# M2 accumulated onto M1's copy in PSUM, M5 kept in C22's place, W1's blocks read into `tv`, and U's dots moved behind its C22 addition

## The chip, the cores and the metric

The kernel runs on one core of a Trainium2 chip. The metric is the device time of one execution in microseconds; lower is better. Before the change it is 2272.84 us, the median of three runs (2270.68 to 2274.14).

## The reference, cut to what matters

The program runs two graph layers on 32 independent graphs ("batches" below) of 512 nodes with 512 features. All numbers are fp32.

```python
h = relu(layernorm(x))
deg = adj.sum(-1)
x = x + relu(concat([h, (adj @ h) / max(deg, eps)]) @ W.T)            # layer 0
h = relu(layernorm(x))
q, k = split(h @ Wqk)
v = h @ Wv
w = scale * mask * ((q * (adj @ (k * mask[:, None]))).sum(-1))        # one score per node
x = x + softmax(w)[:, None] * v                                       # layer 1
```

The kernel rearranges this. Layer 0 becomes `Y = h @ W2` and `o = h @ W1 + (adj/deg) @ Y`. In layer 1 the two weight halves of `Wqk` are multiplied once at the start, so `T = h1 @ (Wq Wk^T)`, `V = h1 @ Wv`, `U = adj/deg @ (h1 * mask)`, and a node's score is the dot product of its row of `T` with its row of `U`, times its degree and mask.

## The kernel before

**Work.** Every 512x512 product is done by one level of Strassen-Winograd: seven products M1 to M7 of 256x256 blocks in place of eight, and additions that combine them. A result has four blocks C11, C12, C21, C22. The sums of operand blocks are written into extra "slots" next to the four blocks (`left_sums`, `right_sums`), by VectorE (DVE).

**Stages.** For each batch `i` four stages run one after the other on TensorE (PE): `layer0_y` makes Y, `layer0_out` makes `o` and adds it to x, `layer1_tv` makes T and V of the batch before, and `layer1_u` makes U. T and V have a second level of Strassen over the weight side, and lie together in one tile `tv` of [128, 2, 2, 14, 128]: the third index is 0 for T and 1 for V. Here "h1 WqWk" in the change's name is the T half, `tv[:, :, 0]`.

**`product`** (line 118) is the common body of Y, o and U. In the kernel before it runs M1, M2, M6, M5, M7, M3, M4. M1, M6, M7 and M4 add up in one PSUM bank `pp`; M2 has a bank `pr`; M5 and M3 share a bank `pq`. Each running sum that a result block needs is copied out of PSUM by ScalarE (ACT, `copy`, line 100), and the block's other part is added by DVE (`add`, line 94; `sub` is line 97). For C22, both M5 and the sum after M7 are copied out by ACT and then added by DVE from SBUF. In `layer0_out` each M has two terms, first `h @ W1`, then `(adj/deg) @ Y`, eight TensorE instructions each; in the trace every matmul of the source shows up as two.

**Order of the work.** Nothing is scheduled by the compiler: the order of the instructions on each engine is the order in which the program emits them. A stage is a Python generator that yields after each group of matmuls, and `run(phase, n, plan)` calls, after step `n` of the stage, whatever `plan.at(n, ...)` has put there, in the order in which it was put. So a plan decides where an addition, a reduction or a load stands in the queue of its engine. Each of these queues (PE, DVE, ACT, GpSimd = POOL, and SP, which issues nearly all loads and stores) runs in order.

**The attention of the batch before** is done by a class `Post`: `recombine` (seven additions on `tv`), `dot` (line 611, four dots of rows of T and U), `scores` and `maximum` (DVE lines 616 and 617, then a reduction over partitions on GpSimd, line 620), `shift` (L623), `exponents` (ACT, L626), `row_sum` (DVE L629, then a second reduction over partitions on GpSimd, L630), `weights` (DVE, L633 and L634), and then V is scaled (`apply`, ACT L638), x is added by a DMA with accumulation that GpSimd issues (`add_x1`, L645), and the rows are stored. `FrontA.factor` (L337) is a small product of degrees and mask on GpSimd; GpSimd also does the power in `variance` (L246).

In `layer0_y` of batch i+1 the plan puts `shift` at step 0, `exponents` at 1, `row_sum` at 2, `FA[i].factor` at 2 (put there after `row_sum`), `weights` at 4, and the recombination of V at 3 to 6. In `layer1_u` the plan puts the recombination of T at 1 and 2, two dots each at 3 and 4, `scores` and `maximum` at 5.

**W1.** The seven blocks of W1 with their sums are kept in device memory[...]; `Stream` reads them again for each batch into four rotating buffers of their own, four at the start of `layer1_u` and three during `layer0_out`.

**PSUM.** All eight banks come from one pool, `ps_m`.

Of the kernel before, what the change touches and what calls it, by code (L numbers as in the profile page):

```python
# [11 lines left out]
F32 = mybir.dt.float32  # L12
# [4 lines left out]
P = 128  # L17
# [5 lines left out]
def kernel(  # L23
# [32 lines left out]

    nc = tc.nc
    B, N, F = x.shape  # L60
    C = N // P
# [7 lines left out]
    big = ctx.enter_context(tc.tile_pool(name="big", bufs=1))  # L69
    small = ctx.enter_context(tc.tile_pool(name="small", bufs=2))  # L70
    dram = ctx.enter_context(tc.tile_pool(name="dram", bufs=2, space=bass.MemoryType.DRAM))
    ps_m = ctx.enter_context(tc.tile_pool(name="ps_m", bufs=8, space=bass.MemoryType.PSUM))


    LEFT = {1: 0, 2: 1, 3: 2, 4: 3, 5: 4, 6: 5, 7: 6}
# [3 lines left out]

    PLACE = {2: 0, 3: 1, 4: 2, 7: 3, 1: 4, 6: 5, 5: 6}  # L80
    AT = {p: j for j, p in PLACE.items()}
    ORDER = [1, 2, 6, 5, 7, 3, 4]

    def slots(tag, bufs, name, pool=None):
        return (pool or big).tile([P, 7, 2, H], F32, tag=tag, bufs=bufs, name=name)

    def block(name):
        return big.tile([P, 2, H], F32, tag="tmp", bufs=4, name=name)

    def mm_tile(name):  # L90
        return ps_m.tile([P, 2, H], F32, tag="m", name=name)

    def add(o, a, b, on=None):
        (on or nc.vector).tensor_tensor(o, a, b, op=ALU.add)  # L94
# [4 lines left out]
    def copy(o, i):  # L99
        nc.scalar.activation(o, i, AF.Copy)  # L100
# [14 lines left out]
    def of(t):  # L115
        return lambda i: t[:, i]

    def product(name, terms, place, finish):

        def m(k, p, first):
            n = 0
            for lt, rt in terms:
                right = rt(k)
                for rc in range(2):
                    for dk in range(2):
                        nc.tensor.matmul(  # L130
                            p[:, rc, :],
                            lt[:, LEFT[k], dk, ts(rc, P)],
                            right[:, dk, :],
                            start=first and n == 0,
                            stop=True,
                            skip_group_check=True,
                        )
                        n += 1
                yield

        pp = mm_tile(f"pp_{name}")
        yield from m(1, pp, True)
        c11 = place(0, 0)
        copy(c11, pp)
        pr = mm_tile(f"pr_{name}")
        yield from m(2, pr, True)
        finish(0, 0, c11, pr, c11)
        yield from m(6, pp, False)
        c12 = place(0, 1)
        copy(c12, pp)  # L150
        pq = mm_tile(f"pq_{name}")
        yield from m(5, pq, True)
        m5 = block(f"m5_{name}")
        copy(m5, pq)
        yield from m(7, pp, False)
        c22 = place(1, 1)
        copy(c22, pp)
        finish(1, 1, c22, m5, c22)
        yield from m(3, pq, False)
        finish(0, 1, c12, pq, c12)  # L160
        yield from m(4, pp, False)
        finish(1, 0, None, pp, None)
# [14 lines left out]
    class Later:  # L177


        def __init__(self, tiles, c):  # L180
            self.tiles, self.c = tiles, c
# [218 lines left out]
    class Stream:  # L400


        def __init__(self):
            self.d = dram.tile([7, P, 2, H], F32, tag="dw1", bufs=1, name="dw1")
            self.tiles = []
            self.n = 0

        def load(self):
            k = ORDER[self.n % 7]
            t = big.tile([P, 2, H], F32, tag="w1", bufs=4, name=f"w1_{self.n}")  # L410
            nc.sync.dma_start(out=t, in_=self.d[RIGHT[k]])
            self.tiles.append((k, t))
            self.n += 1

        def take(self, k):
            want, t = self.tiles.pop(0)
            assert want == k
            return t

    def into(t):  # L420

# [8 lines left out]

    def layer0_y(b):
        y = Y[b] = slots("yh", 1, f"y_{b}")
        return product(f"y_{b}", [(hT, right(w2R))], *into(y))

    def layer0_out(b, w1):
        def place(r, c):
# [14 lines left out]
    def layer1_tv(b):  # L451

        t = TV[b] = tv
        left = H1T[b]

        def m(k, banks, first):
            for half in ((2, 1), (3, 0)):
                for n in half:  # L460
                    if first:
                        banks[n] = mm_tile(f"ptv_{b}_{k}_{n}")
                    for i, p in enumerate(range(2 * n, min(2 * n + 2, 7))):
                        j = AT[p]
                        nc.tensor.matmul(  # L465
                            banks[n][:, :, ts(i, P)],
                            left[:, LEFT[k], LEFT_IN[j], :],
                            mvR[:, RIGHT[k], RIGHT[j], :, :],
                            start=first and i == 0,
                            stop=True,  # L470
                            skip_group_check=True,
                        )
# [12 lines left out]
        def keep(o):  # L485
            return lambda n, p: copy(part(o, n), p)

        def plus(o):
            return lambda n, p: add(part(o, n), p, part(o, n))

        pp, pr, pq, m5 = {}, {}, {}, {}

        def keep5(n, p):
            m5[n] = block(f"m5_tv_{b}_{n}")[:, :, 0:P * min(2, 7 - 2 * n)]
            copy(m5[n], p)

        yield from parts(1, pp, True, keep(0))
        yield from parts(2, pr, True, plus(0))
        yield from parts(6, pp, False, keep(1))
        yield from parts(5, pq, True, keep5)  # L500
        yield from parts(7, pp, False, lambda n, p: add(part(3, n), p, m5[n]))
        yield from parts(3, pq, False, plus(1))
        yield from parts(4, pp, False, keep(2))

    def layer1_one(b, which, held=None):
# [40 lines left out]
        def plus(o):  # L546
            return lambda n, p: add(part(o, n), p, part(o, n))

        pp, pr, pq, m5 = {}, {}, {}, {}

        def keep5(n, p):
            m5[n] = like(n, block(f"m5_w_{which}_{b}_{n}").rearrange("p a f -> p (a f)"))
            copy(m5[n], p)

        yield from parts(1, pp, True, keep(0))
        yield from parts(2, pr, True, plus(0))
        yield from parts(6, pp, False, keep(1))
        yield from parts(5, pq, True, keep5)
        yield from parts(7, pp, False, lambda n, p: add(part(3, n), p, m5[n]))
        yield from parts(3, pq, False, plus(1))  # L560
        yield from parts(4, pp, False, keep(2))

# [16 lines left out]
    class Post:  # L579
# [167 lines left out]
    def start():  # L747
# [42 lines left out]
            for k in range(2):  # L790
                turn_right(s2[h], h, k, w2R)
        for c in range(C):
            v = block(f"h_{c}").rearrange("p a f -> p (a f)")
            nc.scalar.activation(
                in_order(v), natural(X[0][:, c, :]), AF.Relu, scale=t[1][:, c:c + 1], bias=t[2][:, c:c + 1]
            )
            turn_chunk(v, c, "h")
# [7 lines left out]
        rows = {}  # L805

        def scale_a(c):
            rows[c] = block(f"a_{c}").rearrange("p a f -> p (a f)")
            nc.scalar.activation(
                in_order(rows[c]), natural(fa.n[c // 2][:, c % 2, :]), AF.Copy, scale=fa.rdeg[:, c:c + 1]  # L810
            )
# [122 lines left out]
    with tc.manual_schedule(engines=engines):  # L934
        weights, mvR = start()
        post = None
        for i in range(B):
# [4 lines left out]
            if i > 0:  # L942

                p = Plan()
                for n in range(3):
                    p.at(2 * n + 1, stream.load)
                right_y = right_sums(of(Y[i]))
                p.at(0, right_y[0])
                p.at(0, right_y[2])
# [45 lines left out]
                p.at(12, f.stats, 0)  # L995
                p.at(12, f.stats, 1)
                p.at(13, variance, f.t, 0, 2)
                run(layer0_out(i, stream.take), 14, p)


                post = Post(i - 1, F1[i - 1])
# [55 lines left out]
            if more:  # L1057
                p.at(0, f.turn, 0)
                p.at(1, f.turn, 1)
                p.at(2, FA[i + 1].to.read, 0)  # L1060
                p.at(3, FA[i + 1].to.read, 1)
                for n in range(4):
                    p.at(0, stream.load)
            if i == 0:
                fh = FH[2]
                for c in range(C):
# [4 lines left out]
            elif more:  # L1071
                for k in range(7):
                    p.at(1 + k // 4, post.recombine, k, 1, 0)
                for c in range(C):
                    p.at(3 + c // 2, post.dot, c)
                p.at(5, post.scores)
                p.at(5, post.maximum)
                if i == 1:
                    for c in range(C):
                        p.at(3 + c, fa.sum, c)  # L1080
# [24 lines left out]
            if more:  # L1105
# [3 lines left out]
                p.at(3, fb.turn, 1)  # L1109
                p.at(4, fb.sums, 0)  # L1110
                p.at(4, fb.sums, 2)
                p.at(1, load_x, i + 1)
                if i + 2 < B:
                    p.at(5, FH[i + 2].to.read, 0)
                if i > 0:
                    p.at(0, post.shift)
                    p.at(1, post.exponents)
                    p.at(2, post.row_sum)
                    p.at(4, post.weights)
                    for k in range(7):  # L1120
                        p.at(3 + k // 2, post.recombine, k, None, 1)
                p.at(2, FA[i].factor)
# [84 lines left out]
```

## Time and profile before

| | |
|---|---|
| median of three runs | 2272.84 us |
| the profiled execution | 2273.22 us, of which the span from the first to the last instruction is 2271.4 us |
| TensorE clock granted | 0.999 |
| PE busy | 2259.1 us, 99% of the span |
| weight loads of PE busy | 1978.7 us, 87% |
| DVE busy | 1923.6 us, 85% |
| ACT busy | 1025.6 us, 45% |
| POOL busy | 174.8 us, 8% |
| DMA | 463.68 MB, 204 GB/s over the span |

The profile is one execution. Times in it are counted from the first instruction. A busy share is the time in which an engine ran at least one instruction; matmuls overlap each other, so the mean duration of one (379 ns) is longer than the time from one to the next. A timeline row is: start in us, duration in us, engine, source line, operation, output<-input with buffer numbers left out, shapes, how many were merged into the row, and in brackets how long the engine sat idle before it and what ended that. In the list of groups the columns are: line, engine, operation, names, shapes and count, then total busy us and mean ns of one, then the idle time of the engine just before them with what ended most of it.

### The profile page before, as it was taken

To read this page: it belongs to the slowest core of one execution; us is meant where nothing else is said; L and a number is where in the kernel's file an instruction comes from. 1 tells how busy PE (TensorE), PEld (TensorE's weight loads), DVE (VectorE), ACT (ScalarE), POOL (GpSimd) and SP (SyncE) were. 2 spreads that over 40 slices of the span, in tenths; PEclk is the share of its full clock that TensorE was granted. 3 is DMA by queue.
4 is the path that set the end of the run, shared out by engine and by line. 5 is a ranking of instruction groups with operands and counts; after the bars stand their busy time and mean duration, and the time that the engine had idled before them with its cause. 6 is when DMAs were issued, how large, how long until landed. Compare 5 with 4: busy or idle time off the path is not lost.

```text
span 2271.4 us, 32927 instructions
## 1 busy us (share of the span) xinstructions
PE 2259.1 (99%) x10550; PEld 1978.7 (87%) x10550; DVE 1923.6 (85%) x3803; ACT 1025.6 (45%) x1896; POOL 174.8 (8%) x260
## 2 busy tenths in 40 slices
PE   9999999999999999999999999999999999999998
PEld 7788888888888888888888888888888888888897
DVE  7798888888888888888888888888888888888778
ACT  4454443445434554444454344544444543445323
POOL 0000010000100000100000000000000010000000
PEclk9999999999999999999999999999999999999999
DMA  9978787887878777777878888777888787878543
GB/s 222 233 214 246 204 212 193 205 230 206 210 199 202 213 220 207 208 191 207 227 210 205 199 201 218 218 207 202 196 210 225 209 209 193 205 219 217 154 123 96
DMA packets 409773, 463.68 MB, mean 204 GB/s; under 512 B 37729, under 2 KB 271713, under 8 KB 405377
## 3 DMA queue, kind: packets, MB, share of 16 engines
q1 hardware_dynamic: 400192, 428.56, 69.5%
q0 software_dynamic: 8928, 32.51, 8.7%
q8 instruction: 83, 1.36, 0.3%
q14 instruction: 90, 0.73, 0.1%
q10 hardware_dynamic: 480, 0.52, 0.1%
HBM read 293.93 MB, written 167.51 MB: 203 GB/s over the span
## 4 chain that ended last, share of the span: by engine, by line
PE 93%; DMA 3%; DVE 2%; SPq 1%; ACT 0%; issue 0%; DVEq 0%; POOLq 0%; ACTq 0%
PE ptv L465 28%; PE pp_o L130 18%; PE pp_u L130 9%; PE pq_o L130 9%; PE pp_y L130 9%; PE pq_u L130 5%; PE pr_o L130 5%; PE pq_y L130 5%; PE pr_u L130 2%; PE pr_y L130 2%; PE pw L517 1%; DMA a<-in_adj_dram 1%; SPq L212 0%; DVE tv L94 0%; DMA room<-in_L_gnn_Wqk_dram 0%; DVE mv L97 0%
## 5 line engine op out<-in xcount | busy, mean ns | idle before, releaser
L465 PE MATMUL ptv<-mv,h1T 128*128 128x256 f32 x2940 | 639.7, 379 | 0.1
L465 PEld LDWEIGHTS ptv<-mv,h1T 128*128 128x128 f32 x2940 | 558.5, 190 | 76.4 <-DVE xu L444 0.5
L94 DVE TENSOR_TENSOR tv<-tv 128x256 f32<-128x256 f32 (+1 forms) x658 | 326.4, 508 | 13.4 <-ACT tv L100 1.5
L100 ACT ACTIVATE tv<-ptv 128x512 f32<-128x512 f32 (+1 forms) x360 | 184.9, 541 | 262.9 <-PE ptv L465 262.0
L130 PE MATMUL pp_y<-wide 128*128 128x256 f32 x1024 | 242.1, 379 | 1.5 <-ACT y L100 1.2
L130 PE MATMUL pp_u<-h1m,aT 128*128 128x256 f32 x1024 | 242.0, 379 | 0.0
L130 PE MATMUL pp_o<-y,aT 128*128 128x256 f32 x1024 | 241.9, 379 | 0.0
L130 PE MATMUL pp_o<-w,wide 128*128 128x256 f32 x992 | 234.3, 379 | 0.0
L130 PEld LDWEIGHTS pp_y<-wide 128*128 128x128 f32 x1024 | 194.2, 190 | 28.5 <-ACT y L100 1.6
L130 PEld LDWEIGHTS pp_u<-h1m,aT 128*128 128x128 f32 x1024 | 194.4, 190 | 27.0 <-issue 0.7
L130 PEld LDWEIGHTS pp_o<-y,aT 128*128 128x128 f32 x1024 | 194.5, 190 | 26.4
L130 PEld LDWEIGHTS pp_o<-w,wide 128*128 128x128 f32 x992 | 188.5, 190 | 25.6
L100 ACT ACTIVATE o<-pp_o 128x512 f32<-128x512 f32 x96 | 57.2, 596 | 296.0 <-PE pp_o L130 296.0
L100 ACT ACTIVATE y<-pp_y 128x512 f32<-128x512 f32 x128 | 76.3, 596 | 234.5 <-PE pp_y L130 233.4
L94 DVE TENSOR_TENSOR tv<-ptv,tv 128x512 f32<-128x512 f32 x240 | 139.6, 613 | 43.7 <-PE ptv L465 38.4
L97 DVE TENSOR_TENSOR h1T<-h1T 128x512 f32<-128x512 f32 (+2 forms) x193 | 165.8, 873 | 1.2
L100 ACT ACTIVATE xu<-pp_u 128x512 f32<-128x512 f32 x128 | 76.4, 597 | 195.9 <-PE pp_u L130 195.9
L246 POOL TENSOR_TENSOR rstd<-rstd,mhalf 128x2 f32<-128x2 f32 (+1 forms) x96 | 78.7, 820 | 651.0 <-DVE rstd L245 651.0
L130 PE MATMUL pq_y<-wide 128*128 128x256 f32 x512 | 121.0, 379 | 0.0
L130 PE MATMUL pq_o<-y,aT 128*128 128x256 f32 x512 | 121.0, 379 | 0.0
L130 PE MATMUL pq_u<-h1m,aT 128*128 128x256 f32 x512 | 121.0, 379 | 0.0
L94 DVE TENSOR_TENSOR tv<-ptv,m_tv 128x512 f32<-128x512 f32 (+1 forms) x120 | 72.0, 622 | 55.6 <-PE ptv L465 55.1
(130 smaller groups left out, 3269.4 us busy)
## 6 DMA issues: line engine op xcount, KB each, us to landing
w<-dw SPq DMA_DIRECT2D x217, 256.0 KB, 4.3
xu<-in_x_dram SPq DMA_DIRECT2D x128, 256.0 KB, 5.3
a<-in_adj_dram SPq DMA_DIRECT2D x256, 128.0 KB, 3.0
dh1T<-h1m SPq DMA_DIRECT2D x128, 256.0 KB, 3.1
dx<-xu SPq DMA_DIRECT2D x32, 1024.0 KB, 5.1
sh1T<-dh1T SPq DMA_DIRECT2D x256, 128.0 KB, 3.3
shT<-dhT SPq DMA_DIRECT2D x248, 128.0 KB, 6.0
daT<-a SPq DMA_DIRECT2D x124, 256.0 KB, 3.0
```

The costliest lines, as they stand in the source:

```text
L94: (on or nc.vector).tensor_tensor(o, a, b, op=ALU.add)
L97: (on or nc.vector).tensor_tensor(o, a, b, op=ALU.subtract)
L100: nc.scalar.activation(o, i, AF.Copy)
L130: nc.tensor.matmul(p[:, rc, :], lt[:, LEFT[k], dk, ts(rc, P)], right[:, dk, :], start=first and n == 0, stop=True, skip_group_check=True,)
L246: nc.gpsimd.tensor_tensor(rstd[:, a:b], rstd[:, a:b], mhalf[:, a:b], op=ALU.pow)
L465: nc.tensor.matmul(banks[n][:, :, ts(i, P)], left[:, LEFT[k], LEFT_IN[j], :], mvR[:, RIGHT[k], RIGHT[j], :, :], start=first and i == 0, st ...
L517: nc.tensor.matmul(banks[n][:, ts(i, P)], held[:, s, :] if held is not None and j == 3 else left[:, s, LEFT_IN[j], :], mvR[:, RIGHT[k], RI ...
```

## The change

Four edits.

1. **M2 onto M1's copy.** A second PSUM pool `ps_r` takes one of the eight banks. In `product`, ACT copies M1 out of `pp` into this bank `pr` rather than into C11's place, and M2 adds onto it there. C11 is then complete in PSUM: `finish(0, 0, None, pr, None)` copies it to Y or U with ACT, or, for `o`, goes straight to the addition to x. The order becomes M1, M5, M6, M2, M7, M3, M4. The first Y of the program (`seed=False`) still copies and adds. In `layer1_tv` one of M2's and one of M5's four banks is taken from `ps_r`.
2. **M5 in C22's place.** ACT copies M5 directly into C22's place, and DVE adds the sum after M7 to it from PSUM, so that this sum isn't copied. The same in `layer1_tv` and `layer1_one`, where M5 was already copied by ACT into a separate block and the sum was already added from PSUM.
3. **W1's blocks in `tv`.** The four buffers of `Stream` are gone, and the scratch blocks `tmp` are two, not four. The seven blocks of W1 are read into the T half of `tv`, one at each step of `layer0_y`. At the start of the program the rows of h and adj are staged there too.
4. **Plans.** In `layer1_u` the dots move from steps 3 and 4 to 5 and 6, and `scores` and `maximum` from 5 to 6. In `layer0_y`, `shift`, `exponents`, `row_sum` and `weights` move from steps 0, 1, 2, 4 to 1, 2, 3, 5. `FA[i].factor` stays at step 2.

```diff
-    ps_m = ctx.enter_context(tc.tile_pool(name="ps_m", bufs=8, space=bass.MemoryType.PSUM))
+    ps_m = ctx.enter_context(tc.tile_pool(name="ps_m", bufs=7, space=bass.MemoryType.PSUM))
+    ps_r = ctx.enter_context(tc.tile_pool(name="ps_r", bufs=1, space=bass.MemoryType.PSUM))
...
-    ORDER = [1, 2, 6, 5, 7, 3, 4]
+    ORDER = [1, 5, 6, 2, 7, 3, 4]
...
-        return big.tile([P, 2, H], F32, tag="tmp", bufs=4, name=name)
+        return big.tile([P, 2, H], F32, tag="tmp", bufs=2, name=name)
...
+    def seed_tile(name):
+        return ps_r.tile([P, 2, H], F32, tag="r", name=name)
...
         pp = mm_tile(f"pp_{name}")
         yield from m(1, pp, True)
-        c11 = place(0, 0)
+        pr = seed_tile(f"pr_{name}")
+        c11 = pr if seed else place(0, 0)
         copy(c11, pp)
-        pr = mm_tile(f"pr_{name}")
-        yield from m(2, pr, True)
-        finish(0, 0, c11, pr, c11)
+        pq = mm_tile(f"pq_{name}")
+        yield from m(5, pq, True)
+        c22 = place(1, 1)
+        copy(c22, pq)
         yield from m(6, pp, False)
         c12 = place(0, 1)
         copy(c12, pp)
-        pq = mm_tile(f"pq_{name}")
-        yield from m(5, pq, True)
-        m5 = block(f"m5_{name}")
-        copy(m5, pq)
+        yield from m(2, pr, not seed)
+        if seed:
+            finish(0, 0, None, pr, None)
+        else:
+            finish(0, 0, c11, pr, c11)
         yield from m(7, pp, False)
-        c22 = place(1, 1)
-        copy(c22, pp)
-        finish(1, 1, c22, m5, c22)
+        finish(1, 1, c22, pp, c22)
         yield from m(3, pq, False)
         finish(0, 1, c12, pq, c12)
         yield from m(4, pp, False)
...
-        def load(self):
-            k = ORDER[self.n % 7]
-            t = big.tile([P, 2, H], F32, tag="w1", bufs=4, name=f"w1_{self.n}")
-            nc.sync.dma_start(out=t, in_=self.d[RIGHT[k]])
+        def slot(self, k):
+            n = 2 * ORDER.index(k)
+            return tv[:, :, 0, n:n + 2, :].rearrange("p r i f -> p r (i f)")
+
+        def load(self, n):
+            nc.sync.dma_start(out=self.slot(ORDER[n]), in_=self.d[RIGHT[ORDER[n]]])
...
-                        banks[n] = mm_tile(f"ptv_{b}_{k}_{n}")
+                        banks[n] = (seed_tile if n == 0 and k != 1 else mm_tile)(f"ptv_{b}_{k}_{n}")
...
-        yield from parts(5, pq, True, keep5)
-        yield from parts(7, pp, False, lambda n, p: add(part(3, n), p, m5[n]))
+        yield from parts(5, pq, True, keep(3))
+        yield from parts(7, pp, False, plus(3))
...
-                for n in range(3):
-                    p.at(2 * n + 1, stream.load)
...
-                for n in range(4):
-                    p.at(0, stream.load)
...
                 for c in range(C):
-                    p.at(3 + c // 2, post.dot, c)
-                p.at(5, post.scores)
-                p.at(5, post.maximum)
+                    p.at(5 + c // 2, post.dot, c)
+                p.at(6, post.scores)
+                p.at(6, post.maximum)
...
+                for n in range(7):
+                    p.at(n, stream.load, n)
                 p.at(1, load_x, i + 1)
                 if i + 2 < B:
                     p.at(5, FH[i + 2].to.read, 0)
                 if i > 0:
-                    p.at(0, post.shift)
-                    p.at(1, post.exponents)
-                    p.at(2, post.row_sum)
-                    p.at(4, post.weights)
+                    p.at(1, post.shift)
+                    p.at(2, post.exponents)
+                    p.at(3, post.row_sum)
+                    p.at(5, post.weights)
                     for k in range(7):
                         p.at(3 + k // 2, post.recombine, k, None, 1)
                 p.at(2, FA[i].factor)
```

More of the change, by code (lines that the diff above doesn't have):

```diff
@@ L116, in of, with product @@
         return lambda i: t[:, i]
-    def product(name, terms, place, finish):
+    def product(name, terms, place, finish, seed=True):
         def m(k, p, first):
@@ L404, in __init__ @@
             self.d = dram.tile([7, P, 2, H], F32, tag="dw1", bufs=1, name="dw1")
-            self.tiles = []
-            self.n = 0
-        def load(self):
-            k = ORDER[self.n % 7]
-            t = big.tile([P, 2, H], F32, tag="w1", bufs=4, name=f"w1_{self.n}")
-            nc.sync.dma_start(out=t, in_=self.d[RIGHT[k]])
[L412 to L418, printed above, removed]
+        def slot(self, k):
[3 more added lines that the diff above has]
+            nc.sync.dma_start(out=self.slot(ORDER[n]), in_=self.d[RIGHT[ORDER[n]]])
     def into(t):
@@ L432, in layer0_y @@
         y = Y[b] = slots("yh", 1, f"y_{b}")
-        return product(f"y_{b}", [(hT, right(w2R))], *into(y))
+        return product(f"y_{b}", [(hT, right(w2R))], *into(y), seed=b > 0)
     def layer0_out(b, w1):
@@ L489, in plus @@
             return lambda n, p: add(part(o, n), p, part(o, n))
[L491 to L495, printed above, removed]
+        pp, pr, pq = {}, {}, {}
         yield from parts(1, pp, True, keep(0))
@@ L547, in plus @@
             return lambda n, p: add(part(o, n), p, part(o, n))
[L549 to L553, printed above, removed]
+        pp, pr, pq = {}, {}, {}
         yield from parts(1, pp, True, keep(0))
@@ L557, in layer1_one @@
         yield from parts(6, pp, False, keep(1))
-        yield from parts(5, pq, True, keep5)
-        yield from parts(7, pp, False, lambda n, p: add(part(3, n), p, m5[n]))
+        yield from parts(5, pq, True, keep(3))
+        yield from parts(7, pp, False, plus(3))
         yield from parts(3, pq, False, plus(1))
@@ L792, in start @@
         for c in range(C):
-            v = block(f"h_{c}").rearrange("p a f -> p (a f)")
+            v = tv[:, c // 2, 0, 4 * (c % 2):4 * (c % 2) + 4, :].rearrange("p i f -> p (i f)")
             nc.scalar.activation(
@@ L807, in scale_a @@
         def scale_a(c):
-            rows[c] = block(f"a_{c}").rearrange("p a f -> p (a f)")
+            rows[c] = tv[:, c // 2, 1, 4 * (c % 2):4 * (c % 2) + 4, :].rearrange("p i f -> p (i f)")
             nc.scalar.activation(
@@ L997 @@
                 p.at(13, variance, f.t, 0, 2)
-                run(layer0_out(i, stream.take), 14, p)
+                run(layer0_out(i, stream.slot), 14, p)
                 post = Post(i - 1, F1[i - 1])
```

## The prediction

> **What bounds the kernel now.** I read the page's busy times and its chain first.
>
> ```profile
> PE 2259.1 (99%) x10550; PEld 1978.7 (87%) x10550; DVE 1923.6 (85%) x3803; ACT 1025.6 (45%) x1896; POOL 174.8 (8%) x260
> PE 93%; DMA 3%; DVE 2%; SPq 1%; ACT 0%; issue 0%; DVEq 0%; POOLq 0%; ACTq 0%
> ```
>
> PE sets the end. Whether it has gaps is read from the chain in order of time, here one batch:
>
> ```profile
> 1023.35 21.15 PE ptv L465 x98
> 1068.67 3.45 PE pp_o L130 x16
> 1092.85 7.34 PE ptv L465 x34
> ```
>
> A batch takes 1092.85 - 1023.35 = 69.50 us and has 322 matmuls (98 in T and V, 56 in Y, 112 in o, 56 in U): 0.2158 us each, the pace inside one row (3.45/16). There is no gap, and every batch from 165 us on has this period. Lighter DVE or ACT work therefore gains nothing here; a new wait on PE is paid 30 times.
>
> So I looked for what is late where the plans move something. POOL's timeline around Y:
>
> ```profile
> 1056.58 0.38 POOL L620 PARTITION_ALL_REDUCE gtop<-top  x1 [29.72 <-DVE top L617]
> 1062.20 0.39 POOL L630 PARTITION_ALL_REDUCE gs<-es  x1 [5.24 <-DVE es L629]
> 1069.95 0.70 POOL L337 TENSOR_TENSOR wd<-deg,mraw 128x4 f32<-128x4 f32 x1 [7.36 <-DMA shT<-dhT]
> ```
>
> After the second reduction over partitions POOL sits idle for 7.36 us before a product whose inputs are long there; the DMA named has nothing to do with it. The lines' own views and the groups say what it is:
>
> ```profile
> L337 POOLq MODIFY_POOL_CONFIG  x60: 83/83/83, 161.5 to 2174.5; - x60
> L620 POOLq MODIFY_POOL_CONFIG  x62: 6/11/11, 137.4 to 2208.7; - x62
> L337 POOL TENSOR_TENSOR wd<-deg,mraw 128x4 f32<-128x4 f32 x32 | 11.2, 349 | 225.3 <-DMA shT<-dhT 125.7 <-issue 99.6
> ```
>
> Going from the reductions to ordinary arithmetic, POOL reconfigures (30 times, two records each), and likewise on the way back (31 times). The 30 gaps before L337 sum to 225.3 us: 7.51 each. The way back is hidden today: it follows the last power of a batch (1026.86) and the reduction comes 29.7 us later.
>
> DVE's timeline in Y shows what stands behind the softmax sum:
>
> ```profile
> 1065.72 0.16 DVE L633 RECIPROCAL rs<-gs 128x1 f32<-128x1 f32 x1
> 1065.92 0.23 DVE L634 TENSOR_SCALAR sm<-e,rs 128x4 f32<-128x4 f32 x1
> 1066.05 1.41 DVE L94 TENSOR_TENSOR tv<-tv 128x512 f32<-128x512 f32 x2
> 1067.38 0.68 DVE L94 TENSOR_TENSOR y<-m_y,y 128x512 f32<-128x512 f32 x1
> 1067.98 1.41 DVE L94 TENSOR_TENSOR tv<-tv 128x512 f32<-128x512 f32 x2
> 1069.31 0.68 DVE L94 TENSOR_TENSOR y<-pq_y,y 128x512 f32<-128x512 f32 x1
> 1069.91 0.68 DVE L94 TENSOR_TENSOR tv<-tv 128x512 f32<-128x512 f32 x1
> 1070.51 1.41 DVE L97 TENSOR_TENSOR y<-y 128x512 f32<-128x512 f32 x2
> ```
>
> [...]
>
> **The change, part by part.**
>
> *M2 onto M1's copy.* Gone are 96 DVE additions (31 in Y, 32 in U, 32 in o, 1 in the last V) at 0.685 us: 66 us of DVE. New are 63 ACT copies of C11 at 0.596: 38 us of ACT. A copy from PSUM into PSUM has no row; I take 0.6, and even doubled it is hidden, since M5 and M6 (3.45 us in Y and U) lie before M2. Both are worth 0 behind the gapless PE.
>
> *M5 in C22's place.* 97 ACT copies at 0.596 go (58 us, worth 0). The addition costs the same from PSUM (682 ns against 684). But M4 now waits for DVE to have read M7's sum, where it waited for ACT. Cover is M3, 1.73 us in U and Y, 3.45 in o. U: M7 ends at 1053.13, DVE's recombinations, rid of one addition, at 1052.4; the addition runs 1053.24 to 1053.93, M4 is due at 1054.70: 0.7 us to spare. Y: M7 ends 1065.22; DVE reaches the addition at about 1065.15; done 1066.0, M4 due at 1066.78: 0.7 to spare. Cost 0; each us of lateness beyond that costs 31 us a stage. In o over 1.5 us remain.
>
> *W1 into `tv`.* Still 7 loads of 256 KB a batch, from the SP queue. The first waits for the dots (about 1057) and holds back four x loads for normalising and the four of the next x by about 2 us; they are first used after 1077. It lands 4.3 us after issue, near 1061.5, needed at 1068.51; the last is issued by 1066 and needed at 1089. Cost 0.
>
> *Plans.* GpSimd's order in Y was gs, wd. `row_sum` moves from step 2 to 3 and `factor` stays at 2, so it becomes wd, gs: reduction, product, reduction, and the built program has 60 reconfigurations more. Step by step, on the old grid:
> - Dots stand behind C22's addition: C22 at 1053.24, two dots, C12's addition, two dots at 0.61 each end at 1056.9; `scores` ends 1057.33 (1056.37 before); gtop ends 1057.9.
> - Reconfiguration 7.51 and wd (0.35 mean): 1065.8.
> - Back again. This one has no duration in the trace: at least about 0, at most 17.8 (smallest gap in which it is hidden, in front of gtop at 2226.30). I take the opposite direction's 7.51 as the nearest row[...]. 1073.3, and gs ends at 1073.7. (es itself is ready by 1061.2.)
> - rs starts at 1073.75. From rs to the end of Y's first right-hand sum the rows above take 1071.19 - 1065.72 = 5.47; C22's addition (0.60) and one pair of `tv` additions (1.33) now stand before rs, leaving 3.54: 1077.3.
> - That sum is C12 - C11, which M5 of o multiplies. M5 used to be fourth; it is second now, and its Y term takes the place of M2's, which started at 1073.69.
>
> PE waits 3.66 us per batch, in the 30 batches with a `Post` in Y: 110 us. DVE's idle time rises there, but what follows on it is due later by the same 3.66. A third reconfiguration, before o's first power, starts at about 1078 behind the accumulating DMAs and ends at 1085.5; the power is due near 1089. Hidden.
>
> *Start.* In Y of batch 0, M5 needs four DVE sums, not three: about +0.5. In U of batch 0, M4 (79.89) must now wait for C22's addition, and the trace has DVE waiting for data there:
>
> ```profile
> 81.10 1.30 DVE L283 STREAM_TRANSPOSE h1T<-sh1T 128x512 f32<-128x512 f32 x2 [3.62 <-DMA sh1T<-dh1T]
> 89.86 1.99 PE L130 MATMUL pp_y<-wide 128*128 128x256 f32 x8 [1.18 <-ACT y L100]
> ```
>
> Transposes until 82.33, three statistics (0.8 each), the addition: M4 at 85.5, +5.6; the later wait at 89.86 (1.3 with what the overlap hides) is absorbed. +4.8 in all at most; if the data land earlier without W1's four loads beside them, +1.5. I take +3.3. *End.* The last U's C22 addition ended at 2239.78, now 2239.2, against M4 at 2237.92: +1.3 on PE; DVE, busy to the end, loses V's C11 addition, -0.7. +0.7.
>
> Sum 110 + 3.3 + 0.7 = 114 on the span of 2271.4 (execution 2273.22); on the median of 2272.84 this is **2387 us**.
>
> **Rivals.**
> A. As above[...].
> B. The other side: returning to the reductions' code is short. Below about 3.85 us gs is there early enough that M5 never waits, and 4 us remain: 2277, not measurably slower. For it: the records of that direction last 11 ns, not 83, and no gap shows its price. Against: at the start, too, the first special operation came 7.4 us after its configuration.
> C. DVE is late for C22's addition in Y or U, and M4 waits. For: 0.7 us to spare on an engine 85% busy, more if waits between dependent additions add up. Against: it loses 2 us of work a batch. At 1 us late in both stages 0.3 x 2 x 31 = 19 us more: 2406; without A, 2296.
> D. W1's blocks are late: bandwidth near Y rises by 1.8 MB in 14 us. It would take 7 us of delay to touch M1; each us beyond costs 31.
>
> **How the numbers follow.** A 0.80, B 0.08, C on top 0.09, D 0.03. Slower 0.92, same 0.06 (most of B), faster 0.02; 0.2% (4.5 us) is about what a measurement can tell from no change. A's own range is 2335 to 2430; B lies below it and little above, so 2325 to 2430 leaves out less than 2 in 10.
>
> **What would show it.** Right: POOL's rows in Y in the order gtop, wd, gs with about 7.5 us before each of the last two; DVE idle some 7 us before rs, released by POOL; PE idle 3 to 4 us in front of M5's Y term (pq_o from y), released by DVE; a period near 73.2. Wrong: gs within 4 us after wd (B); waits of pp_u or pp_y on DVE in every batch (C), or of pp_o and pq_o on a DMA (D).

## The result, and the profile after

| | before | after |
|---|---|---|
| median, 4 runs of each side by side | 2273.36 us (2270.68 to 2274.14) | 2378.18 us (2375.5 to 2382.22) |
| span of the profiled execution | 2271.4 us | 2376.3 us |
| TensorE clock granted | 0.999 | 0.992 |

The ratio is 1.0465, with a 95% interval of 1.0447 to 1.0483: the change makes the kernel 4.65% slower. The forecast was 2387 us, with a range of 2325 to 2430.

The page's busy times and its chain, for the kernel after:

```profile
PE 2285.9 (96%) x10550; PEld 1987.2 (84%) x10550; DVE 1878.0 (79%) x3707; ACT 1013.3 (43%) x1862; POOL 170.5 (7%) x260
PE 73%; issue 9%; DVE 9%; DMA 5%; SPq 2%; POOL 1%; ACT 1%; DVEq 0%; POOLq 0%; ACTq 0%
```

PE has as many instructions as before (10550), but its share of the chain falls from 93% to 73%. DVE and ACT are lighter, as the change makes them, and it buys nothing. The list of PE's waits, its three largest (what waited, what it waited for: us in total, how often, the longest), says where PE stands:

```profile
PE pq_o L136 <- DVE y L103: 73.2, 30, 5.1
PE pp_u L136 <- DVE xu L100: 5.2, 2, 4.0
PE pp_v L136 <- DVE v L100: 1.7, 1, 1.7
```

Before, no batch in the steady part had a wait. Now 30 batches wait in one place, M5's Y term in `o` (`pq_o`), for Y's first right-hand sum on DVE. No batch waits for a DMA. Follow one batch backwards, first PE's timeline after:

```profile
1117.29 1.89 PE L136 MATMUL pq_o<-tv,wide 128*128 128x256 f32 x8
1121.32 1.99 PE L136 MATMUL pq_o<-y,aT 128*128 128x256 f32 x8 [2.14 <-DVE y L103]
```

M5's W1 term starts at 1117.29 and fills 8 x 0.2158 = 1.73 us, so the Y term could start at 1119.02; it starts 2.30 us later. DVE's timeline:

```profile
1110.65 0.69 DVE L100 TENSOR_TENSOR y<-pp_y,y 128x512 f32<-128x512 f32 x1 [0.30 <-PE pp_y L136]
1117.71 0.16 DVE L626 RECIPROCAL rs<-gs 128x1 f32<-128x1 f32 x1 [6.37 <-POOL gs L623]
1120.58 1.41 DVE L103 TENSOR_TENSOR y<-y 128x512 f32<-128x512 f32 x2
```

DVE makes the addition into C22 on time (0.30 us idle, waiting for PE), then stands 6.37 us in front of `rs`. The first of the two sums at 1120.58 is ready at 1121.26, and PE starts 0.06 us after that. POOL's timeline says why `rs` is late:

```profile
1102.90 0.38 POOL L613 PARTITION_ALL_REDUCE gtop<-top  x1 [29.61 <-DVE top L610]
1110.89 0.20 POOL L344 TENSOR_TENSOR wd<-deg,mraw 128x4 f32<-128x4 f32 x1 [7.60 <-DVE tv L100]
1117.27 0.40 POOL L623 PARTITION_ALL_REDUCE gs<-es  x1 [6.19 <-issue]
```

The order is now gtop, wd, gs, with an idle stretch in front of each of the last two. The groups give the sum of those stretches:

```profile
L623 POOL PARTITION_ALL_REDUCE gs<-es x32 | 12.8, 402 | 195.0 <-issue 190.4 <-DVE es L622 4.5
L344 POOL TENSOR_TENSOR wd<-deg,mraw 128x4 f32<-128x4 f32 x32 | 6.3, 196 | 232.3 <-DMA xu<-in_x_dram 109.9 <-DVE tv L100 87.6 <-issue 17.8
```

The way back to the reductions, which no row of the kernel before priced, costs 190.4 / 30 = 6.35 us.

One thing is there that the prediction did not have. In some batches the matmuls behind the stall are slow:

```profile
1698.97 2.76 PE L136 MATMUL pq_o<-y,aT 128*128 128x256 f32 x8 [2.77 <-DVE y L103]
1701.52 2.85 PE L136 MATMUL pp_o<-tv,wide 128*128 128x256 f32 x8
1704.21 1.89 PE L136 MATMUL pp_o<-y,aT 128*128 128x256 f32 x8
```

Eight matmuls take 1.89 us from the first start to the last end, and 2.76 and 2.85 in these two groups. Matmul by matmul, 7 or 8 of them follow each other at 0.43 us instead of 0.2158: half pace. This happens behind 9 of the 30 stalls.

The trace also records the clock that TensorE was granted. A row of the next view is a stretch (from:to), its length, the busy us and instructions of PE, PEld, DVE, ACT and POOL in it, then the granted clock (1.00 is full), the DMA share and GB/s:

```profile
1696.64:1700.05 3.41, 1.08 (x5) 0.98 (x6) 3.38 (x6) 0.72 (x1) 0.69 (x1) 1.00 0.76 170
1700.05:1703.46 3.41, 3.41 (x10) 2.67 (x9) 3.38 (x7) 1.70 (x3) 0.37 (x1) 0.50 0.73 108
1703.46:1706.88 3.42, 3.42 (x17) 3.00 (x17) 3.38 (x6) 0.72 (x2) 0.86 (x1) 1.00 0.67 109
```

So the slow matmuls are a clock of one half, granted for 3.41 us, and not late operands. Each of the nine has such a stretch in the record; between the first product of T and V and the last matmul there is no other.

**Where the 104.9 us of span went**, counted from one matmul's start to the next: 5.6 up to the first product of T and V; 78.1 in the 30 stalls (2.60 each, 1.72 to 5.23); 19.7 between the stalls; and 1.5 at the end. Of the 19.7 about 16 are the nine stretches at half pace (1.8 each), 2 are a second matmul that starts 0.1 us late after each of the other stalls, and 1.5 are M4 in `o`, which starts up to 0.3 us late in nine batches because it waits for the addition into C22.

### The profile page after: what moved, and what is told of

Its sections match the earlier page's. It is cut to its first block, busy times and chain, and to the rows that moved or that the text cites. A ratio compares the mean times of both kernels' runs of the same rounds, so it can differ in the third digit from the quotient of the medians.

```text
span 2376.3 us, 33129 instructions
## 1 busy us (share of the span) xinstructions
PE 2285.9 (96%) x10550; PEld 1987.2 (84%) x10550; DVE 1878.0 (79%) x3707; ACT 1013.3 (43%) x1862; POOL 170.5 (7%) x260
## 4 chain that ended last, share of the span: by engine, by line
PE 73%; issue 9%; DVE 9%; DMA 5%; SPq 2%; POOL 1%; ACT 1%; DVEq 0%; POOLq 0%; ACTq 0%
PE ptv L466 27%; PE pp_o L136 14%; PE pp_u L136 9%; PE pq_o L136 8%; PE pr_o L136 5%; PE pq_u L136 4%; DVE tv L100 4%; DMA xu<-in_x_dram 3%; PE pp_y L136 2%; PE pr_u L136 2%; PE pq_y L136 2%; DVE y L103 1%; DVE y L100 1%; PE pw L514 1%; SPq L211 1%
## 5 line engine op out<-in xcount | busy, mean ns | idle before, releaser
L106 ACT ACTIVATE tv<-ptv 128x512 f32<-128x512 f32 x480 | 240.7, 546 | 230.4 <-PE ptv L466 223.7
L100 DVE TENSOR_TENSOR tv<-ptv,tv 128x512 f32<-128x512 f32 (+1 forms) x360 | 212.3, 617 | 77.2 <-PE ptv L466 67.2
L136 PE MATMUL pp_o<-tv,wide 128*128 128x256 f32 x992 | 242.2, 388 | 0.0
L136 PEld LDWEIGHTS pp_o<-tv,wide 128*128 128x128 f32 x992 | 194.0, 196 | 31.1 <-DVE o L100 2.7
L136 PE MATMUL pq_o<-y,aT 128*128 128x256 f32 x512 | 132.7, 405 | 73.2 <-DVE y L103 73.2
L263 ACT ACTIVATE n<-n,nmr,rstd 128x512 f32<-128x512 f32 x120 | 88.3, 803 | 241.3 <-DVE nmr L257 241.3
L136 PEld LDWEIGHTS pq_o<-y,aT 128*128 128x128 f32 x512 | 99.0, 198 | 98.5 <-DVE y L103 85.3
L626 DVE RECIPROCAL rs<-gs 128x1 f32<-128x1 f32 x32 | 5.2, 163 | 200.1 <-POOL gs L623 200.1
L136 PE MATMUL pq_o<-tv,wide 128*128 128x256 f32 x496 | 117.2, 379 | 0.0
```

The lines of the kernel that those rows point to most:

```text
L136: nc.tensor.matmul(p[:, rc, :], lt[:, LEFT[k], dk, ts(rc, P)], right[:, dk, :], start=first and n == 0, stop=True, skip_group_check=True,)
L263: nc.scalar.activation(o, i, AF.Relu, scale=t[1][:, c:c + 1], bias=t[2][:, c:c + 1])
L626: nc.vector.reciprocal(self.rs, self.gs)
```

## Experiments

Theory T: the two reconfigurations ahead of gs hold up `rs`, DVE stands there with Y's right-hand sums queued behind it, and M5's Y term, now second in `o`, waits for them. The rivals: the order of the products by itself, W1's loads or the additions into C22, and the reconfigurations by some other way than DVE.

### GpSimd's order turned back

```diff
-                p.at(2, FA[i].factor)
+                p.at(3, FA[i].factor)
```

> The changed kernel with one call moved: the product wd is planned one step later in Y, so GpSimd's order is the old one again (gtop, gs, wd); M's order, the seed in PSUM, W1 in tv and the dots are as changed. Theory T (two reconfigurations ahead of gs hold up rs, Y's first right-hand sum and so the second product of o): the 105 us above the kernel before shrink to those of the start (5.6) and of the end (about 1.4), 2280 us (2276 to 2285); no wait of pq_o on DVE's y; the matmuls at half pace in o are gone, since they stand only behind those waits. Rival M (M5 in second place, whatever GpSimd does): unchanged near 2378, pq_o still waiting. Rival W (W1's loads in Y, or the additions into C22 that M4 waits for): unchanged near 2378.

Measured: 2280.95 us, ratio to before 1.0031 (1.0020 to 1.0042). PE's largest wait in this run:

```profile
PE pp_u L136 <- DVE xu L100: 5.2, 2, 4.0
```

That is the start and the end. `pq_o` is gone from the list, from the second period on every one is 69.50 us, and there is no half pace in any of them. The one call accounts for 97 of the 105 us. What is left is the start (6.3 in this run) and the end (1.5). GpSimd's reconfiguration is still there, but where it was: 9.35 us idle in front of wd in one batch, behind gs, with nobody waiting. Neither M's new order, nor W1's loads, nor the C22 additions cost anything in the period.

### The late reduction kept, DVE's wait moved

```diff
                 if post is not None:
+                    p.at(1, post.weights)
                     for c in range(C):
...
-                    p.at(5, post.weights)
```

> The changed kernel with GpSimd's late gs kept (gtop, wd, gs, all 60 added reconfigurations) but with DVE's two instructions behind it (rs, sm) moved from Y to o, behind Y's right-hand sums. Theory T (the loss is DVE standing at rs in front of those sums): 2280 us (2276 to 2292) as with the order turned back, and no wait of pq_o on y. Rival R (the reconfigurations themselves, or GpSimd's lateness on any other way, cost the time): near 2378.

Measured: 2283.56 us, ratio 1.0044 (1.0029 to 1.0059). POOL's and DVE's timelines of this run, one batch:

```profile
1071.83 0.45 POOL L344 TENSOR_TENSOR wd<-deg,mraw 128x4 f32<-128x4 f32 x1 [8.28 <-DMA xu<-in_x_dram]
1078.58 0.40 POOL L623 PARTITION_ALL_REDUCE gs<-es  x1 [6.31 <-issue]
```

```profile
1074.06 1.41 DVE L103 TENSOR_TENSOR y<-y 128x512 f32<-128x512 f32 x2
1079.02 0.16 DVE L626 RECIPROCAL rs<-gs 128x1 f32<-128x1 f32 x1 [1.02 <-POOL gs L623]
```

GpSimd does what it does in the changed kernel, both reconfigurations in sight and gs no earlier. But Y's sums now stand ahead of `rs`, and PE no longer waits for them. The median is 2.6 us above that of the run before, whose interval overlaps with this one. So the reconfigurations cost next to nothing by themselves; they cost what stands behind the instruction that waits for their result.

### GpSimd's order alone, on the kernel before

```diff
+                p.at(2, FA[i].factor)
                 if i > 0:
                     p.at(0, post.shift)
...
-                p.at(2, FA[i].factor)
```

> The kernel before with that one part of the change alone: wd ahead of the reduction gs (gtop, wd, gs), everything else old, so that M2 is second in o, M6 third and M5 fourth. Theory T: gs comes about 5.8 us later (7.6 + 0.2 + 6.35 behind gtop), rs near 1071.5 on the old grid, the second right-hand sum (M6's factor) ready near 1077.7 where it is due at 1077.14: 0.6 us a batch in 30 batches, 2290 us (2273 to 2310), with a wait of M6's Y term (pp_o) on DVE's y if any. Rival G (the GpSimd order costs what it costs whatever the order of the products, for instance through DVE's own delay): the whole loss, 2365 to 2378.

Measured: 2344.12 us, ratio 1.0310 (1.0293 to 1.0328). A miss: 71 us, not 17, though the wait is at the place named. PE's waits, and the rows of POOL and PE of one batch:

```profile
PE pp_o L130 <- DVE y L97: 40.6, 29, 3.1
PE ptv L465 <- DVE xu L444: 11.2, 25, 0.5
```

```profile
1019.65 0.38 POOL L620 PARTITION_ALL_REDUCE gtop<-top  x1 [27.30 <-DVE top L617]
1027.40 0.19 POOL L337 TENSOR_TENSOR wd<-deg,mraw 128x4 f32<-128x4 f32 x1 [7.38 <-DMA xu<-in_x_dram]
1033.40 0.40 POOL L630 PARTITION_ALL_REDUCE gs<-es  x1 [5.80 <-issue]
```

```profile
1029.87 1.89 PE L130 MATMUL pp_o<-w,wide 128*128 128x256 f32 x8
```

gtop starts 10.22 us ahead of `o`'s first product here. In the kernel before this product started at 1068.51, and gtop 1068.51 - 1056.58 = 11.93 us ahead of it:

```profile
1068.51 1.89 PE L130 MATMUL pp_o<-w,wide 128*128 128x256 f32 x8
```

The dots themselves are 1.71 us late against PE. My estimate took them to be on the old grid. DVE's work is 1913.9 / 32 = 59.8 us a batch, and it stands 193.1 / 30 = 6.4 at `rs`: 66.2 of a period of 69.5. That leaves little for its other waits, and DVE is also late for the relu additions of `o` (`ptv` waits for them in 25 batches), and for the next dots; that the one comes of the other is put to the test in the next run. By start-to-start times the stalls of M6's Y term sum to 45.4 us, those of T and V to 18.5, and what follows the former to 9.7 (four stretches at half pace among it); together 73.6, against 72.9 us of span.

What this means for theory T: my explanation that M5's second place is what makes it bite was too strong. In the old order of products the same GpSimd order costs 71 us, in the new one 97.

### The same, with DVE's wait moved

On the kernel of the last run:

```diff
                 if post is not None:
+                    p.at(1, post.weights)
                     for c in range(C):
...
-                    p.at(4, post.weights)
```

> The kernel before with wd ahead of gs, as in the run of that one part, and with rs and sm moved from Y to o behind Y's right-hand sums. That run took 2344 us where 2290 was expected: gtop itself came 1.9 us later against TensorE's work than in the kernel before. Theory D (DVE, 60 us of work a batch, cannot make up the 6.7 us it stands at rs in a period of 69.5, so it is late for the next batch's first matmul of T and V, and for the dots, and the delay feeds itself): with DVE freed from that wait all of it goes, 2275 us (2272 to 2284). Rival G (GpSimd's order delays the dots or T and V in another way): 2300 or more.

Measured: 2275.2 us, ratio 1.0010 (1.0003 to 1.0017). Waits on DVE's y and the repeated waits of `ptv` are gone; one wait of 2.6 us is left, in the profiled execution, which with 2281.96 us is the slowest of 20. So DVE's stand at `rs` is the whole loss there too, but for some 2 us, its knock-on into the next batch included.

### Work put into the stall

```diff
         pq = mm_tile(f"pq_{name}")
+        if name.startswith("o_") and name != "o_0":
+            lt, rt = terms[0]
+            for rc in range(2):
+                for dk in range(2):
+                    nc.tensor.matmul(
+                        pq[:, rc, :], lt[:, LEFT[5], dk, ts(rc, P)], rt(5)[:, dk, :],
+                        start=rc == 0 and dk == 0, stop=True, skip_group_check=True,
+                    )
         yield from m(5, pq, True)
```

> The changed kernel with 8 matmul records more in each o but batch 0's: M5's first term (h with W1) is done twice, the second time from a cleared bank, so the result is the same. That is 1.73 us of TensorE work put where it stands idle for 2.6 us (1.7 to 5.2) in 30 batches. Theory T+H (the stall is bounded by DVE, so work put into it is free; and the matmuls at half pace behind some stalls come of the idle time, which falls to about 0.9 us): the stall of pq_o falls by 1.7, the 19.7 us of half pace go, 2360 us (2355 to 2368), faster than the changed kernel with more work in it. Rival N (half pace has another cause): unchanged near 2378. Rival P (TensorE was not really idle there): 30 x 1.73 = 52 us more, 2430.

Measured: 2370.89 us, ratio 1.0434 (1.0419 to 1.0450), 7 us less than the changed kernel. One batch on PE, where L157 holds the added matmuls, and the wait in total:

```profile
1049.33 1.89 PE L157 MATMUL pq_o<-tv,wide 128*128 128x256 f32 x8
1051.06 1.89 PE L136 MATMUL pq_o<-tv,wide 128*128 128x256 f32 x8
1053.53 1.99 PE L136 MATMUL pq_o<-y,aT 128*128 128x256 f32 x8 [0.59 <-DVE y L103]
```

```profile
PE pq_o L136 <- DVE y L103: 27.1, 28, 3.6
```

Some 52 us of TensorE work went in and the time did not rise: PE was idle there, and DVE sets the end of the stall. That the kernel got faster is likely but not certain, since the two intervals against the kernel before touch (1.0450 and 1.0447). The profile is of the slowest of the four executions (2376.65 us). In it stretches at half pace fell from 9 to 2. The size was missed: the expectation gave all 19.7 us to half pace, of which 16 are, and the wait fell by 46 us, not 52. The other 6 go with a later gs: the gaps in front of wd sum to 238.2 us here and to 232.3 in the changed kernel. And M4 of `o` waits for its C22 addition in three batches, 2.7 us.

### A longer stall

```diff
-            nc.gpsimd.tensor_tensor(W[self.b], DEG[self.b], mraw[:, :, self.b], op=ALU.mult)
+            for _ in range(11 if 0 < self.b < 31 else 1):
+                nc.gpsimd.tensor_tensor(W[self.b], DEG[self.b], mraw[:, :, self.b], op=ALU.mult)
```

> The changed kernel with the product wd made 11 times over in the 30 batches concerned: 10 more GpSimd instructions of about 0.2 us between gtop and gs, 2.0 us in each batch. Theory T (gs, rs and Y's first right-hand sum hold up M5 directly): each stall of pq_o grows from 2.6 to about 4.6 us, 60 us more, 2438. Theory T+H (half pace follows with a chance that rises with the idle time): beside that nearly all of the 30 stalls instead of 9 are followed by 8 slow matmuls (1.8 to 2.0 us each), 2475 us (2455 to 2485). Rival S (DVE gives part of the time back, or some of the wait is hidden): under 2430.

Measured: 2504.88 us, ratio 1.1014 (1.0999 to 1.1029). POOL's and PE's timelines and the wait in total:

```profile
1170.21 3.00 POOL L345 TENSOR_TENSOR wd<-deg,mraw 128x4 f32<-128x4 f32 x11 [7.88 <-issue]
```

```profile
1183.42 3.78 PE L136 MATMUL pq_o<-y,aT 128*128 128x256 f32 x8 [5.11 <-DVE y L103]
```

```profile
PE pq_o L136 <- DVE y L103: 151.1, 30, 7.9
```

Eleven products take 3.00 us, so ten more cost (3.00 - 0.20) / 10 = 0.28 each, not the 0.20 of their busy time. From start to start the stalls grew from 78.1 to 156.0 us, 2.6 a batch for 2.8 added. Next to nothing is given back, which excludes rival S. All 30 stalls (4.3 to 8.1 us) are now followed by half pace, and what follows them costs 67 us instead of 18. 78 + 49 = 127 are the whole difference between the two profiles; most of the 30 us by which the expectation was low are the 0.28 (18) and longer stretches at half pace than I took (6 to 14 matmuls, not 8).

### Everything mended

GpSimd's ordinary work is put together (the core of the edit), and DVE's order at both ends changed:

```diff
-                if last:
-                    p.at(1, FA[i].factor)
+                p.at(1, FA[i].factor)
...
-        for f in r2[:3] + l0[:3] + r2[3:] + l0[3:]:
-            f()
+        for k in (0, 2, 1):
+            r2[k]()
+            l0[k]()
+        l0[3]()
+        r2[3]()
...
-                p.at(0, f.turn, 0)
-                p.at(1, f.turn, 1)
+                p.at(5 if i == 0 else 0, f.turn, 0)
+                p.at(5 if i == 0 else 1, f.turn, 1)
...
-                    p.at(2 + c, fh.stats, c)
-                p.at(5, variance, fh.t)
+                    p.at(5 + c // 2, fh.stats, c)
+                p.at(6, variance, fh.t)
...
-                    p.at(4 + k // 2, f.inner_sums, k, 2, 7, s4)
+                    p.at(5 + k // 2, f.inner_sums, k, 2, 7, s4)
...
-                p.at(2, FA[i].factor)
+                if i == 0:
+                    p.at(2, FA[i].factor)
...
-        p.at(4, final.weights)
-        p.at(4, final.finish, 0, 0)
+        p.at(5, final.weights)
+        p.at(5, final.finish, 0, 0)
```

> The changed kernel with wd made in T and V right behind the power (GpSimd's ordinary work all together, so no reconfiguration at all between gtop and gs), and with DVE's order changed at both ends: at the start the sums that M5 and M6 use come first, and in U of batch 0 the transposes and statistics stand behind the addition into C22; in the last U two of H1's inner sums, and in the last V the weights and the first result block, stand behind that addition. Theory T (nothing of the change but GpSimd's order and the two ends costs time): 2273 us (2268 to 2277), a period of 69.50 throughout, the same as the kernel before. Rival: some cost of the change is left in every batch, 2280 or more.

Measured: 2278.52 us, ratio 1.0021 (1.0013 to 1.0028); just above what T gave. Waits in the profile of this run:

```profile
PE pp_y L136 <- DVE y L100: 4.4, 3, 2.3
PE pp_o L136 <- ACT o L106: 2.4, 1, 2.4
```

At the end PE no longer waits (from the last U's first matmul to the last matmul 34.9 us, before 35.0), and what follows the last matmul is 7.7 us long, before 8.8. U of batch 0 no longer waits; the first matmul of Y of batch 1 comes at 83.47 (before 81.61, changed kernel 88.42). But time is lost elsewhere at the start. M4 of the very first Y waits 2.3 us for its C22 addition (changed kernel 0.7), the longest of the three waits of `pp_y`. Then M4 of Y of batch 1 waits for the C22 addition behind DVE's sums of weights, and M7 of `o` waits for ACT, which sat in front of a row sum of adj whose load was late. So one further run:

```diff
-                        p.at(3 + k, weights[k])
+                        p.at(4 + k if k < 3 else 6, weights[k])
...
-                            p.at(2 + 2 * h + c, fa.sum, 2 * h + c)
-                            p.at(8 + 2 * h + c, fa.write, 2 * h + c)
-                        p.at(5 + 2 * h, fa.degrees, h)
+                            p.at(6 + h, fa.sum, 2 * h + c)
+                            p.at([10, 11, 12, 12][2 * h + c], fa.write, 2 * h + c)
+                        p.at(8 + 2 * h, fa.degrees, h)
```

> The last kernel, with everything mended (2278.5 us), and two more moves at the start: one of DVE's weight sums behind the addition into C22 in Y of batch 1 (TensorE stood 1.5 us in front of M4 there), and in o of batch 1 ACT's row sums of adj, which wait for a load, behind the copy of C12 (2.6 us, and about 1.5 us of half pace behind it). Theory T (what is left of the change's cost is the order of DVE and ACT in the first batches, nothing in the period): 2273 us (2271 to 2276), a first product of T and V near 120.5 instead of 125.8. Rival L (the start is bound by loads that the change delays, W1's among them): 2276 or more, the wait reappears at another tile.

Measured: 2275.38 us, ratio 1.0009 (1.0002 to 1.0016). The first product of T and V starts at 122.5 (before 119.3, changed kernel 125.0); the 3.2 us to the kernel before are all lost ahead of U of batch 0, whose first matmul comes at 72.5 (before 69.1, changed kernel 70.7), so the stages behind it lose nothing more. The trace has them at M4 of the very first Y:

```profile
29.65 3.43 PE L136 MATMUL pp_y<-wide 128*128 128x256 f32 x8 [2.12 <-DVE y L100]
```

It waits 2.12 us for its C22 addition, and eight matmuls take 3.43 us instead of 1.89, in a half-clock stretch that the record has at 30.05. So rival L was right that the wait reappears at another tile, but what is waited for is the addition, as at the other places, and not a load that the change delays: DVE waits there for a load of W as long as before (1.56 us, before 1.50). M4 of `o` also waits for its C22 addition in three batches, 2.1 us in all. The span of this profile (the slowest of 21 executions) is 3.9 us above the kernel before: 3.2 at the start, 2.0 between, and 1.2 less at the end. So mended, the change costs about 2 us in the medians, and has no gain. None of these kernels beats the one before.

## Why the prediction was right

**Bound.** PE without a gap, a period of 69.50 us, lighter DVE and ACT worth nothing: right. With GpSimd's order turned back DVE still has 40 us less work than before and the period is 69.50 again.

**M2, M5, W1.** Taken as 0: right, each in sight in the run with the order turned back. The C22 additions are on time in every batch between the first and the last, and no product of `o` waits for W1. DVE's busy time fell by 46 us (1923.6 to 1878.0) where the count of additions gave 66; nothing hangs on it behind a gapless PE.

**GpSimd's chain.** The mechanism is right step for step: gtop, wd, gs, DVE standing at `rs`, M5's Y term. From gtop's end to `rs` the prediction had 15.85 us; measured, in the batch shown, 14.43. Two terms were mis-sized: the way back, taken as the opposite direction's 7.51, is 6.35, and wd, taken as the mean of 0.35, is 0.20. From `rs` to the sum 3.54 was forecast; it is 3.55 (1117.71 to 1121.26). So the stall is 2.60 a batch instead of 3.66, 78 us instead of 110. The third reconfiguration, before the power in `o` (POOL sits idle for 8.51 us there in the batch shown, until DVE's input comes), is hidden from PE as forecast: no wait of PE leads to it. The two ends of A's own range, 2335 and 2430, were my estimates of a shorter and a longer way back; the 6.35 is on the shorter side.

**The missing term.** What follows a stall: 19.7 us. The prediction priced a stall by its length only. In the nine stretches at half pace the matmuls follow each other at 0.43 us against 0.2158, and the clock record has 3.41 us for each. The length of the stall alone doesn't tell which are followed by one: a stall of 2.27 us was, and one of 3.43 was not. What sorts them is in the last section. The too long stall and the missing term nearly cancel, 97.8 against 110. That the sum came out within 9 us is in this part luck: had nothing followed the stalls, the forecast would have been some 29 us too high.

**Start.** +3.3 forecast, +5.6 measured, above the +4.8 called the most. M4 of U in batch 0 starts at 85.18, forecast 85.5, so that step was right; it is again what follows the stall (1.6 us at half pace) that was left out, and U's first matmul is 1.5 us later instead of 0.5, because in the first Y not only M5 waits (0.75) but also M4, for its C22 addition (0.70).

**End.** +0.7 forecast, +1.5 measured. M4 of the last U waits 1.3, as forecast. The last V was forecast to win 0.7 back. What follows its last matmul is in fact 1.7 shorter (7.1 us, before 8.8), but M4 there also waits for its C22 addition, 1.8 us, which the forecast did not have.

**Rivals.** B (a short way back) fell with the 6.35. C (C22's additions late in every batch) was not seen in Y or U; the late additions at both ends and the 1.5 us in `o` are of its kind. D (W1 late) was not seen. C's own remark, that waits between dependent additions could add up on a full DVE, comes nearest to what the GpSimd order does to the kernel before, though it is DVE's stand at `rs` that starts it: there it cost 71 us where a count on the old grid gave 17. In the changed kernel, with 79% of DVE taken, gtop starts 10.9 us ahead of `o` where the forecast had 11.0, so that lateness hardly enters.

## What to carry to other kernels

On an engine whose queue runs in order, ask of each instruction that waits for another engine what stands behind it. DVE stood 6.37 us at `rs` with the sums that TensorE needs queued behind it; moving the two instructions that wait (`rs`, `sm`) behind those sums gave back about as much as removing the delay itself (2283.6 us against 2281.0). GpSimd work of one kind belongs together: the product between two reductions made two reconfigurations visible (232.3 / 30 = 7.74 and 190.4 / 30 = 6.35 us of idle time a batch), and made beside the power it needs none there (no idle time in front of it in the run with everything mended). A stall is not priced by its length alone: an engine that was nearly full (DVE with 66.2 us of a period of 69.5, with GpSimd's order alone) carries the delay into the next batch, and TensorE may run at half pace behind it (0.43 us a matmul instead of 0.2158, behind 9 of the 30 stalls).

## What the runs showed that I had not expected

- TensorE at half pace behind short stalls: 9 of 30 with a mean of 2.6 us, 2 of 30 with the stall partly filled (one of 2.02 us), 30 of 30 with stalls of 4.3 us and more, 6 to 14 matmuls long (the clock record has 3.41 or 6.83 us). Of stalls between 2.0 and 3.5 us some have it and some don't, so the length alone doesn't decide.
- What sorts them in the trace of the changed kernel is the place of the stall on a fixed grid of time. In its clock record the half-clock stretches start at 85.55, 181.12, 256.21, 474.67, 1266.56, 1700.05 us and so on, and these starts lie whole multiples of 3.413 us apart (the first two gaps, 95.57 and 75.09, are 28 and 22 of them). If the execution is cut into windows on that grid, each of the nine stalls with half pace puts at least 2.03 us (up to 3.21) of idle time into one window, and none of the other 21 more than 1.94. The stall that ends at 1698.97, 2.93 us long, has 2.33 us in the first window shown in the section on the result. The one that ends at 1920.24 is longer, 3.43 us, but two windows share it about equally, and the clock stays full:

```profile
1915.09:1918.51 3.42, 1.89 (x9) 1.33 (x7) 1.81 (x5) 1.30 (x2) 0.40 (x1) 1.00 1.21 216
1918.51:1921.92 3.41, 1.68 (x8) 1.50 (x9) 3.38 (x6) 0.72 (x1) 1.06 (x1) 1.00 0.67 98
1921.92:1925.33 3.41, 3.41 (x18) 3.00 (x17) 3.38 (x6) 1.82 (x3) 0.86 (x1) 1.00 0.89 141
```

- The most idle time in one window sorts the stalls of the other runs too, those with half pace behind them against those without: 2.19 us and more against 2.00 and less with GpSimd's order alone, 2.02 and more against 1.94 and less with the stall partly filled, 2.82 and more with the longer stall, where all are followed. This is read from the traces afterwards; no run moves a stall against the grid on purpose, so what sets the clock is not shown.
- The reconfiguration of GpSimd isn't the same both ways: 7.51 us of idle time from the reductions to the ordinary product (225.3 / 30 in the kernel before), 6.35 back (190.4 / 30 in the changed kernel).
- Ten small GpSimd products in a row cost 0.28 us each in time, with 0.20 us busy.
